# Two attention layers: each block closed one turn later, and another order in the last turn

## The chip, the cores and the metric

The kernel runs on one core of a Trainium2 chip. The metric is the device time of one execution in microseconds (us); fourteen executions of the kernel before have a median of 4657.06 us (4653.63 to 4668.51). The core's engines work side by side, each through its own queue in order: TensorE (PE, matmuls; PEld its weight loads), VectorE (DVE), ScalarE (ACT), GpSimd (POOL) and SyncE (SP, which only issues transfers). They wait for one another through semaphores.

## What is computed

Eight steps act on a table of 3125 nodes with 256 features: four graph layers and four mixtures of experts in turn. The change touches the third step alone, two graph attention layers over 50000 edges plus one loop for each node. Each layer is

```python
h = (x @ W).reshape(n_nodes, Hh, Cc)          # 4 heads of 64
a_src = (h * att_src).sum(-1)
a_dst = (h * att_dst).sum(-1)
alpha = leaky_relu(a_src[src] + a_dst[dst])
m = jax.ops.segment_max(alpha, dst, num_segments=n_nodes)
e = jnp.exp(alpha - m[dst])
denom = jax.ops.segment_sum(e, dst, num_segments=n_nodes)
w = e / jnp.clip(denom, 1e-16)[dst]
out = jax.ops.segment_sum(w[:, :, None] * h[src], dst, num_segments=n_nodes)
return out.reshape(n_nodes, Hh * Cc) + bias
```

The first layer's result goes through relu into the second; the second's is added to the table. A mixture of eight experts (two for each node) follows.

## The kernel before

Nodes are padded to 25 blocks of 128 (T = 25), and the edges are sorted by receiver, so that block b has 17 chunks of 128 edges (kb = 17, KB = 17), the last block 8. `attend` runs one attention layer; its body is `attend_blocks`. The two large layers take its branch for `small = False` (64 features a head); a third, small layer later in the program takes the other branch, which is not touched.

**The parts of a block's work** (functions inside `attend_blocks`):

- `begin` issues one gather for each chunk on POOL (`self.gather`, L373): 128 rows of the table `rows`, 260 wide, into the tile `ad_rows`, which has four buffers. On SP it loads the block's own rows (`ad_hx`, pool `ad_x`, three buffers) and the receivers' numbers (`ad_rb`).
- `hot`, `hot_t`, `hot_wide` build one-hot matrices of the receivers (DVE; `hot_wide` is an ACT copy to float32, two buffers). `to_edges` brings the receivers' logits to the edges (PE), `receivers` finishes them (DVE).
- `highest` scans the gathered logits along the chunks for the largest of each receiver (DVE, L2279 to L2287) and transposes the ends (PE, L2289). `across` scans over the 128 lanes (DVE, L2294) and transposes back (PE, L2297). `scores` makes the exponents (DVE L2302 to L2315, then ACT's exp L2316).
- `products` multiplies the gathered rows by their weights, a range of chunks at a time (DVE, L2325, four instructions, one for each head).
- `summed(x, j)` adds the products up by receiver with matmuls against the one-hot matrices (PE, L2344), two matmul records a chunk. j counts four ranges of chunks, `x.cut = [0, 2, kb // 2, kb - kb // 4, kb]`.
- `closed` divides by the sum of the weights and adds the node's own loop (DVE, L2353 to L2366, then the first instructions of `finish`). What is left of `finish` is a generator, `x.end`.

`finish` is `to_second` in layer 1: after bias and relu (L2494, L2495), `x.end` runs `heads`: two transposes on PE (L2176), a copy on ACT (L2178), four matmuls (L2182), a copy on ACT (L2184), the store of the block's new row into layer 2's table on SP (L2185), and a copy of eight columns on DVE (L2186). In layer 2 it is `to_rows`: bias and sum into the table X (L2500, L2501), and `x.end` then sends up to two routed rows on POOL (`mix_send`, L891) and advances the router of the next mixture by one `mix_step` (two in the last blocks). A router group of five blocks takes six steps: mean, variance and normalisation (the first, with L204, which writes one of two row buffers), transposes and logits (L822, L812, read on DVE by L816), the two best experts, counts (L856, L857, read by L872) and positions.

**The order.** `in_order` chains the instructions of PE, of DVE and of ACT in the order in which the program makes them, and the middle of the program is chained on POOL too; SP is not. The loop runs 26 turns. In turn b the block b is `mid` (its logits are scanned), b - 1 is `low` (its products are summed) and b + 1 is `new` (its gathers are issued, its one-hot matrices built). At the end of the turn `low` is closed, the first half of `mid`'s products is made, and `low.end` is run to its end. Between the layers POOL sends 30 records of another graph's sort (`own_send(30)`, L1968), issued behind the last block's gathers of layer 1.

Of the kernel before, what the change touches and what calls it, by code (L numbers as in the profile page):

```python
# [36 lines left out]
T = 25  # L37
# [1236 lines left out]
class Fast(Net):  # L1274
# [920 lines left out]
    def attend_blocks(self, s, C, rows, nd, finish, hxs, spare, tail, between):  # L2195
        nc, tc = self.nc, self.tc
# [3 lines left out]
        small = C < 64  # L2200
        with ExitStack() as ctx:
# [10 lines left out]
            hp = ctx.enter_context(tc.tile_pool(name="ad_h", bufs=4 if small else 2))  # L2212
            fp = None if small else ctx.enter_context(tc.tile_pool(name="ad_f", bufs=2))
            tp = ctx.enter_context(tc.tile_pool(name="ad_t", bufs=2))
            xp = None if small else ctx.enter_context(tc.tile_pool(name="ad_x", bufs=3))
            op = ctx.enter_context(tc.tile_pool(name="ad_o", bufs=2)) if small else None
            psc = ctx.enter_context(tc.tile_pool(name="ad_pc", bufs=1, space=PSUM))
            psx = ctx.enter_context(tc.tile_pool(name="ad_px", bufs=1, space=PSUM))
# [26 lines left out]
            def hot(x, j):  # L2245
                k0 = s.k0[x.b]
                for k in range(j * x.kb // 2, (j + 1) * x.kb // 2):
                    nc.vector.tensor_scalar(x.hb[:, k, :], self.iotab, s.rel[:, k0 + k:k0 + k + 1], None,  # L2248
                                            op0=OP.is_equal)

            def hot_t(x):
                nc.vector.tensor_scalar(x.hT[:, :x.kb * P], x.rb[:, :x.kb * P], self.pcol, None, op0=OP.is_equal)
# [5 lines left out]
            def to_edges(x):  # L2258

                x.px = psx.tile([P, KB, 24], F32, name="ad_px")  # L2260
                for k in range(x.kb):
                    nc.tensor.matmul(x.px[:, k, :], x.hT[:, k * P:(k + 1) * P],
                                     nb[:, x.b].rearrange("p j f -> p (j f)"), start=True, stop=True)
# [11 lines left out]
            def highest(x):  # L2275

                kb = x.kb
                v = sp.tile([P, 4, KB], F32, name="ad_v")[:, :, :kb]
                nc.vector.tensor_copy(v, x.es.rearrange("p k h -> p h k"))  # L2279
                x.F = sp.tile([P, 2, 4, KB], F32, name="ad_F")[:, :, :, :kb]  # L2280
                for h in range(4):
                    nc.vector.tensor_tensor_scan(x.F[:, 0, h, :], s.drop[:, x.ks], v[:, h, :], -BIG, OP.add, OP.max)
                for h in range(4):
                    nc.vector.tensor_tensor_scan(x.F[:, 1, h, ::-1], s.end[:, x.ks][:, ::-1], v[:, h, ::-1], -BIG,
                                                 OP.add, OP.max)
                nc.vector.tensor_copy(e[:, 0:4], x.F[:, 0, :, kb - 1])
                nc.vector.tensor_copy(e[:, 32:36], x.F[:, 1, :, 0])  # L2287
                x.two = psc.tile([P, P + 36], F32, name="ad_pt")
                nc.tensor.transpose(x.two[0:36, 0:P], e, self.ident)  # L2289

            def across(x):

                for q, out, way in ((0, slice(2, P + 2), slice(0, P)), (32, slice(P - 1, None, -1), slice(P - 1, None, -1))):
                    nc.vector.tensor_tensor_scan(c[q:q + 4, out], s.dropT[q:q + 4, x.b, way], x.two[q:q + 4, way], -BIG,  # L2294
                                                 OP.add, OP.max)
                x.pb = x.two[:, P:]
                nc.tensor.transpose(x.pb, c[:, 1:P + 1], self.ident[0:36, 0:36])  # L2297

            def scores(x):
                kb = x.kb  # L2300
                z = x.z[:, :, 0, :]
                nc.vector.tensor_tensor(z, x.es, x.ex[:, :, 4:8], OP.add)  # L2302
                nc.vector.scalar_tensor_tensor(z, z, 0.2, z, op0=OP.mult, op1=OP.max)
                q = sp.tile([P, 4, KB], F32, name="ad_q")[:, :, :kb]
                for i, far in enumerate((s.cum, s.back)):
                    nc.vector.tensor_tensor(q, x.pb[:, 32 * i:32 * i + 4, None].to_broadcast([P, 4, kb]),
                                            far[:, None, x.ks].to_broadcast([P, 4, kb]), OP.add)
                    nc.vector.tensor_max(x.F[:, i], x.F[:, i], q)
                nc.vector.tensor_max(q, x.F[:, 0], x.F[:, 1])
                top = sp.tile([P, KB, 4], F32, name="ad_top")[:, :kb, :]  # L2310
                nc.vector.tensor_max(top, q.rearrange("p h k -> p k h"), x.ex[:, :, 0:4])
                nc.vector.tensor_add(top, top, x.ex[:, :, 4:8])
                nc.vector.scalar_tensor_tensor(top, top, 0.2, top, op0=OP.mult, op1=OP.max)
                nc.vector.tensor_tensor(x.z, x.z, top[:, :, None, :].to_broadcast([P, kb, 2, 4]), OP.subtract)
                nc.vector.tensor_tensor(x.z, x.z, s.mask[:, x.ks, :, None].to_broadcast([P, kb, 2, 4]), OP.add)  # L2315
                nc.scalar.activation(x.rt[:, :kb, W4:HY], x.z.rearrange("p k i h -> p k (i h)"), AF.Exp)  # L2316
# [22 lines left out]
            def summed(x, j):  # L2339
                if j == 0:  # L2340
                    x.acc = psa.tile([P, 3 * HY if small else HY], F32, name="ad_acc")
                for k in range(x.cut[j], x.cut[j + 1]):
                    lhs, rhs = (x.hb, x.rp.rearrange("p k i f -> p k (i f)")) if small else (x.hd, x.rt)
                    nc.tensor.matmul(x.acc, lhs[:, k, :], rhs[:, k, :], start=k == 0, stop=k == x.kb - 1)  # L2344

            def closed(x):
                den = sp.tile([P, 4], F32, name="ad_den")
                o4 = sp.tile([P, 4], F32, name="ad_o4")
                tot = x.acc
                if small:  # L2350
                    tot = sp.tile([P, HY], F32, name="ad_tot")
                    nc.vector.tensor_reduce(tot, x.acc.rearrange("p (i f) -> p f i", i=3), AX.X, OP.add)
                nc.vector.tensor_reduce(den, tot[:, W4:HY].rearrange("p (i h) -> p h i", i=2), AX.X, OP.add)  # L2353
                nc.vector.scalar_tensor_tensor(o4, den, 0.5, tot[:, HX:HY], op0=OP.is_lt, op1=OP.add)
                nc.vector.scalar_tensor_tensor(den, den, 0.5, den, op0=OP.is_lt, op1=OP.add)
                if small:
                    nc.vector.tensor_scalar_add(den, den, 1e-16)
                else:
                    nc.vector.tensor_scalar_max(den, den, 1e-16)
                nc.vector.reciprocal(den, den)  # L2360
                o = op.tile([P, W4], F32, name="ad_out") if small else x.hx[:, 0:W4]
                ov = o.rearrange("p (h c) -> p h c", h=4)
                nc.vector.tensor_tensor(ov, x.hx[:, 0:W4].rearrange("p (h c) -> p h c", h=4),
                                        o4[:, :, None].to_broadcast([P, 4, C]), OP.mult)
                nc.vector.tensor_tensor(o, o, tot[:, 0:W4], OP.add)
                nc.vector.tensor_tensor(ov, ov, den[:, :, None].to_broadcast([P, 4, C]), OP.mult)  # L2366
                x.end = finish(x.b, o)
                next(x.end)
# [8 lines left out]
            if small:  # L2377
# [6 lines left out]
                for b in range(T + 3):  # L2384
                    low, second, first, new = second, first, new, None
# [37 lines left out]
                        pass  # L2423
                return
            mid = low = None
            for b in range(T + 1):
                low, mid, new = mid, new, None
                if b + 1 < T:
                    new = begin(b + 1)
                if mid:  # L2430
                    highest(mid)
                if low:
                    summed(low, 0)
                if new:
                    hot_t(new)
                    to_edges(new)
                if mid:
                    across(mid)
                if low:
                    products(low, low.cut[2], low.kb)  # L2440
                    summed(low, 1)
                if new:
                    hot(new, 0)
                if mid:
                    scores(mid)
                if new:
                    hot(new, 1)
                    hot_wide(new)
                if low:
                    summed(low, 2)  # L2450
                    summed(low, 3)
                if new:
                    receivers(new)
                if low:
                    closed(low)
                if mid:
                    products(mid, 0, mid.cut[2])
                if low:
                    for _ in low.end:
                        pass  # L2460

    def r1_gnn(self):
        nc, tc, a = self.nc, self.tc, self.a
# [487 lines left out]
```

## Time and profile before

| what | value |
|---|---|
| median of 14 executions | 4657.06 us |
| the profiled execution | 4667.21 us, its span 4665.4 us |
| busy over the span | PE 72%, DVE 66%, POOL 47%, ACT 37% |
| mean granted TensorE clock | 0.84 of full |
| layer 1: first to last gather | 1079.6 to 1624.4 us |
| layer 2: first to last gather | 1667.7 to 2249.7 us |
| one turn of layer 1, blocks 3 to 23 | 22.3 us |
| last closing (L2353), layer 1 and layer 2 | 1658.1 and 2296.2 us |

How to read the views: the page's groups give line, engine, operation, output and inputs, count, then busy us and the mean ns of one, then the engine's idle time just ahead of them and what ended it. The timeline gives start, duration, engine, line, operation and, in brackets, the idle time ahead of it and its releaser. The view by windows gives start and end of each, then for PE, PEld, DVE, ACT and POOL the busy us and instruction count, then the granted TensorE clock (1.00 is full), the DMA share and GB/s. The waits give who waited for whom: total us, times, longest.

### The profile page before, as it was taken

The numbers are of one execution on the slowest core, as the hardware profiler recorded it, in microseconds if no ns is written. First come the engines' busy times: TensorE is split into PE (matmuls) and PEld (weight loads), VectorE is DVE, ScalarE is ACT, GpSimd is POOL, SyncE is SP. The second block draws the span as 40 slices with busy tenths as digits, with TensorE's granted clock in tenths as the row PEclk, the third lists the DMA queues.
The fourth block names the chain that finished last, engine by engine and source line by source line (L and its number), as shares of the span: only waits on it lengthen the run. The fifth ranks groups of instructions, "written<-read, shape, count | busy, mean of one in ns | idle before, by whom it ended". The sixth has DMA issues, their size and how long they took to land.

```text
span 4665.4 us, 58758 instructions
## 1 busy us (share of the span) xinstructions
PE 3352.0 (72%) x17877; PEld 2696.3 (58%) x17877; DVE 3081.3 (66%) x10158; ACT 1735.4 (37%) x3743; POOL 2183.7 (47%) x2117
## 2 busy tenths in 40 slices
PE   5689977854566534444475897757688699997998
PEld 2479965743444423433354676644455489876887
DVE  8768874355777758887745787756877789643221
ACT  5736451221111101111111698733233368762221
POOL 2665545566777777777455000027777100022222
PEclk9689987976777767767687998879789799998999
DMA  2942224654554434444355222221111012355665
GB/s 58 213 131 100 100 95 152 188 161 125 139 141 138 123 103 132 131 129 126 98 174 160 71 103 86 72 55 33 38 33 35 8 60 84 119 162 169 190 190 164
DMA packets 345476, 535.49 MB, mean 115 GB/s; under 512 B 78177, under 2 KB 246881, under 8 KB 341878
## 3 DMA queue, kind: packets, MB, share of 16 engines
q1 hardware_dynamic: 249218, 372.22, 25.2%
q0 software_dynamic: 90272, 155.06, 13.7%
q10 hardware_dynamic: 5652, 4.27, 0.3%
q8 instruction: 148, 2.42, 0.2%
q14 instruction: 186, 1.52, 0.1%
HBM read 390.08 MB, written 146.81 MB: 115 GB/s over the span
## 4 chain that ended last, share of the span: by engine, by line
PE 28%; DVE 20%; POOL 14%; issue 10%; DMA 7%; ACT 6%; DVEq 0%; SPq 0%; POOLq 0%; ACTq 0%
POOL ad_rows L373 12%; PE gx_pa L1063 5%; PE gx_po L1003 4%; ACT oo_y L2043 3%; PE ad_acc L2344 3%; PE r_pa L1778 3%; DVE ad_hb L2248 2%; DVE ad_rows L2325 2%; DMA ys<-gx_ys,gx_to 2%; PE r_o L1740 2%; PE ss_sum L2716 2%; DMA ad_rows<-r_rows,fa_gi 2%; PE r_pa L1780 2%; PE r_pa L1781 1%; DMA ad_rows<-q_rows,own_gi 1%
## 5 line engine op out<-in xcount | busy, mean ns | idle before, releaser
L373 POOL DMA_INDIRECT ad_rows<-r_rows,fa_gi x832 | 842.5, 1013 | 280.1 <-issue 240.1
L1968 POOL DMA_INDIRECT os_table<-os_rec,os_at x512 | 564.1, 1102 | 483.3 <-ACT r_wt L1669 135.6
L373 POOL DMA_INDIRECT ad_rows<-q_rows,own_gi x416 | 401.4, 965 | 636.8 <-DMA q_w<-in_L_ffn_W 510.3
L2344 PE MATMUL ad_acc<-ad_rows,ad_hd 128*128 128x264 f32 x1664 | 498.2, 463 | 9.2 <-DVE ad_rows L2325 9.2
L891 POOL DMA_INDIRECT regions<-gh_xn,gd_at x150 | 152.2, 1015 | 629.6 <-PE r_pa L1778 462.7
L2289 PE MATMUL ad_pt<-ident,ad_e 128*36 128x128 f32 x75 | 26.1, 348 | 577.6 <-DVE ad_e L2287 577.6
L1064 ACT ACTIVATE gx_h<-gx_pa,gx_bias 128x256 f32<-128x256 f32 x392 | 185.5, 473 | 673.0 <-PE gx_pa L1063 672.9
L2344 PEld LDWEIGHTS ad_acc<-ad_rows,ad_hd 128*128 128x128 f32 x1664 | 374.4, 232 | 86.2 <-DVE ad_rows L2325 9.9
L1063 PE MATMUL gx_pa<-gx_xt,gx_w 128*128 128x256 f32 x1568 | 388.2, 406 | 42.9 <-DVE gx_xt L1044 40.2
L1003 PE MATMUL gx_po<-gx_w,gx_h 128*128 128x256 f32 x1568 | 371.3, 383 | 27.6 <-DVE gx_ys L1005 27.6
L1063 PEld LDWEIGHTS gx_pa<-gx_xt,gx_w 128*128 128x128 f32 x1568 | 309.9, 202 | 115.8 <-DVE gx_xt L1044 60.8
L2289 PEld LDWEIGHTS ad_pt<-ident,ad_e 128*36 128x36 f32 x75 | 7.8, 104 | 607.8 <-issue 582.1
L1003 PEld LDWEIGHTS gx_po<-gx_w,gx_h 128*128 128x128 f32 x1568 | 294.0, 192 | 70.7 <-DVE gx_ys L1005 31.4
L2316 ACT ACTIVATE ad_rows<-ad_z 128x136 f32<-128x136 f32 (+1 forms) x75 | 23.5, 314 | 805.4 <-DVE ad_z L2315 779.1
L1631 PE MATMUL r_pa<-r_xn,r_wt 128*128 128x257 f32 x1250 | 299.0, 384 | 24.4 <-ACT r_wt L1669 24.4
L2716 PE MATMUL ss_sum<-r_xw,ss_wt 128*128 128x256 f32 x1250 | 288.6, 393 | 0.6 <-DVE r_xw L2609 0.6
L1053 DVE TENSOR_TENSOR gx_to<-gx_tf,gd_other 128x2 int32<-128x2 f32 x84 | 13.5, 161 | 415.3 <-DMA ys<-gx_ys,gx_to 209.6
L2716 PEld LDWEIGHTS ss_sum<-r_xw,ss_wt 128*128 128x128 f32 x1250 | 244.8, 198 | 35.5 <-DVE r_xw L2609 1.0
L1631 PEld LDWEIGHTS r_pa<-r_xn,r_wt 128*128 128x128 f32 x1250 | 229.5, 193 | 53.0 <-ACT r_wt L1669 25.1
L2325 DVE SCALAR_TENSOR_TENSOR ad_rows<-ad_rows 128x512 f32<-128x512 f32 (+2 forms) x400 | 258.8, 709 | 1.5
L1011 POOL DMA_INDIRECT xd<-gx_ys,gx_to x56 | 86.3, 1541 | 333.3 <-DVE gx_ys L1006 267.1
L2856 PE MATMUL q_o<-q_w,q_h 128*128 128x256 f32 x800 | 203.9, 400 | 6.7 <-ACT q_ct L2824 3.4
(615 smaller groups left out, 7913.7 us busy)
## 6 DMA issues: line engine op xcount, KB each, us to landing
gx_w<-in_L_ffn_W SPq DMA_DIRECT2D x56, 1024.0 KB
mats<-r_wt SPq DMA_DIRECT2D x25, 1600.0 KB
ss_wt<-mats SPq DMA_DIRECT2D x25, 1600.0 KB
gx_w<-in_L_ffn_W SPq DMA_DIRECT2D x56, 512.0 KB
regions<-zero SPq DMA_DIRECT2D x26, 1040.0 KB
ad_rb<-fa_relT SPq DMA_DIRECT2D x48, 544.0 KB
gx_xs<-regions SPq DMA_DIRECT2D x84, 260.0 KB
cnts<-r_cb SPq DMA_DIRECT2D x75, 256.0 KB
```

The source lines that it names most:

```text
L373: return self.nc.gpsimd.indirect_dma_start(out=out, out_offset=None, in_=table[:, :], in_offset=bass.IndirectOffsetOnAxis(ap=idx, axis=0))
L891: ins = nc.gpsimd.indirect_dma_start(out=self.regions[:, :], out_offset=bass.IndirectOffsetOnAxis(ap=m.at[i][:, t:t + 1], axis=0), in_=x, ...
L1003: nc.tensor.matmul(po, h[:, f, j * P:(j + 1) * P], w2s[:, f, :], start=f == 0, stop=f == FC - 1)
L1063: nc.tensor.matmul(ps, w1s[:, c, f * P:(f + 1) * P], xt[:, c, :], start=c == 0, stop=c == DC - 1)
L1064: done = nc.scalar.activation(h[:, f, :], ps, act, bias=bias1[:, f, k:k + 1])
L1631: nc.tensor.matmul(pa, wt[:, i, :], xn[:, g * G + i, :], start=i == 0, stop=i == G - 1)
L1778: nc.tensor.matmul(pa, c[:, u - u0, :], xs[:, u, 0:2 * D], start=u == 0, stop=u == T - 1)
L1968: i = nc.gpsimd.indirect_dma_start(out=s.table[:, :], out_offset=bass.IndirectOffsetOnAxis(ap=s.at[:, c:c + 1], axis=0), in_=s.rec[:, c, : ...
L2325: i = nc.vector.scalar_tensor_tensor(rv[:, :, h, :], rv[:, :, h, :], 1.0, x.rt[:, u:v, W4 + h:W4 + h + 1].to_broadcast([P, v - u, C]), op0 ...
L2344: nc.tensor.matmul(x.acc, lhs[:, k, :], rhs[:, k, :], start=k == 0, stop=k == x.kb - 1)
L2716: nc.tensor.matmul(sums[t], wt[:, d, :], xw[:, d, :], start=d == 0, stop=d == T - 1)
L2856: nc.tensor.matmul(po, last[:, c, f * P:(f + 1) * P], w2[:, e - 1, c, :], start=c == 0, stop=c == FC - 1)
```

## The change

A block is closed one turn later: `done` is the block that was `low` in the turn before. Its closing stands behind `highest(mid)`, and its `end` behind `summed(low, 1)`. The pool `ad_x` gets a fourth buffer, since a block's own rows are held longer. In turn T - 1 (24) the two older blocks, 22 and 23, are closed and ended ahead of the scans of block 24. Of block 24 only the first two chunks' products are made in that turn, and they are summed at once; in turn T the other three ranges of chunks are multiplied and summed by turns, and the block is closed.

```diff
-            xp = None if small else ctx.enter_context(tc.tile_pool(name="ad_x", bufs=3))
+            xp = None if small else ctx.enter_context(tc.tile_pool(name="ad_x", bufs=4))
...
             mid = low = None
+            done = None
+
+            def ended(x):
+                closed(x)
+                for _ in x.end:
+                    pass
+
             for b in range(T + 1):
                 low, mid, new = mid, new, None
+                if b == T - 1:
+                    ended(done)
+                    products(low, low.cut[2], low.kb)
+                    for j in range(4):
+                        summed(low, j)
+                    ended(low)
+                    low = done = None
+                if b == T:
+                    for j in range(1, 4):
+                        products(low, low.cut[j], low.cut[j + 1])
+                        summed(low, j)
+                    ended(low)
+                    break
                 if b + 1 < T:
                     new = begin(b + 1)
-                if mid:
-                    highest(mid)
+                highest(mid)
+                if done:
+                    closed(done)
                 if low:
                     summed(low, 0)
                 if new:
                     hot_t(new)
                     to_edges(new)
-                if mid:
-                    across(mid)
+                across(mid)
                 if low:
                     products(low, low.cut[2], low.kb)
                     summed(low, 1)
+                if done:
+                    for _ in done.end:
+                        pass
                 if new:
                     hot(new, 0)
-                if mid:
-                    scores(mid)
+                scores(mid)
                 if new:
                     hot(new, 1)
                     hot_wide(new)
...
                 if new:
                     receivers(new)
-                if low:
-                    closed(low)
-                if mid:
+                if b == T - 1:
+                    products(mid, 0, mid.cut[1])
+                    summed(mid, 0)
+                else:
                     products(mid, 0, mid.cut[2])
-                if low:
-                    for _ in low.end:
-                        pass
+                done = low
```

## Prediction, on record before the result was known

> **What bounds the kernel now.** I read the page first (engines, groups), then the waits inside layer 1, then the timeline of one turn and of the last turns, then the clock by windows. The span is 4665.4 us; its execution took 4667.2 us, 10 us above the median of 4657.1, so the sum is made as a difference and added to either.
>
> The page's group of gathers of the two large layers:
>
> ```profile
> L373 POOL DMA_INDIRECT ad_rows<-r_rows,fa_gi x832 | 842.5, 1013 | 280.1 <-issue 240.1
> ```
>
> Waits of 1166 to 1612 us, twenty turns of layer 1 (total us, times, longest):
>
> ```profile
> POOL ad_rows L373 <- issue: 96.9, 318, 0.3
> DVE ad_v L2279 <- DMA ad_rows<-r_rows,fa_gi: 61.4, 20, 3.7
> DVE r_nd L2186 <- ACT hd_hx L2184: 18.8, 20, 1.5
> ```
>
> POOL never waits for anything but its own 0.3 us between two gathers. A turn lasts 22.3 us (scans of block 3 at 1170.3, of block 23 at 1616.1: 445.8 / 20) because 17 gathers take it. DVE has 3.1 us to spare a turn, idle at L2279 until the rows land, and 0.9 us at L2186. One turn:
>
> ```profile
> 1170.32 0.25 DVE L2279 COPY ad_v<-ad_rows 128x68 f32<-128x68 f32 x1 [2.97 <-DMA ad_rows<-r_rows,fa_gi]
> 1171.92 1.97 PE L2344 MATMUL ad_acc<-ad_rows,ad_hd 128*128 128x264 f32 x4
> 1172.25 0.84 DVE L2294 TENSOR_TENSOR_SCAN ad_c<-fa_dropT,ad_pt 4x128 f32<-4x128 bf16 x2
> 1173.12 2.77 DVE L2325 SCALAR_TENSOR_TENSOR ad_rows<-ad_rows 128x576 f32<-128x576 f32 x4
> 1174.51 8.69 PE L2344 MATMUL ad_acc<-ad_rows,ad_hd 128*128 128x264 f32 x30
> 1183.24 0.17 DVE L2353 TENSOR_REDUCE ad_den<-ad_acc 128x4 f32<-128x8 f32 x1 [0.30 <-PE ad_acc L2344]
> 1188.94 0.17 DVE L2186 COPY r_nd<-hd_ps 128x8 f32<-128x8 f32 x1 [0.31 <-ACT hd_hx L2184]
> ```
>
> PE fills 1171.9 to 1183 without a hole. Its clock, around the scans of block 8 (1281.3), is half and then full:
>
> ```profile
> 1281.30:1287.30 6.00, 4.58 (x27) 3.60 (x28) 5.89 (x22) 0.00 (x0) 4.78 (x5) 0.50 0.63 191
> 1287.30:1297.50 10.20, 6.42 (x29) 4.95 (x28) 9.48 (x42) 2.32 (x2) 7.76 (x9) 1.00 0.39 106
> ```
>
> The end of layer 1, where DVE, not POOL, sets the pace:
>
> ```profile
> 1635.18 0.19 DVE L2279 COPY ad_v<-ad_rows 128x32 f32<-128x32 f32 x1 [0.20 <-issue]
> 1647.48 0.17 DVE L2353 TENSOR_REDUCE ad_den<-ad_acc 128x4 f32<-128x8 f32 x1 [4.29 <-PE ad_acc L2344]
> 1658.11 0.17 DVE L2353 TENSOR_REDUCE ad_den<-ad_acc 128x4 f32<-128x8 f32 x1 [3.13 <-PE ad_acc L2344]
> 1664.51 0.32 SPq L2185 DMA_DIRECT2D r_rows<-hd_hx  x1
> 1667.68 0.99 POOL L373 DMA_INDIRECT ad_rows<-r_rows,fa_gi  x1 [2.68 <-PE ad_px L2262]
> ```
>
> Layer 2 cannot gather until the last block's rows are stored (L2185).
>
> **Part 1, the interior of layer 1.** What goes: DVE's wait at L2353 for the last sums, 2.1 us over twenty turns. It stands beside POOL's gathers, so it buys nothing. What moves: the closing (L2353 to L2495, 1183.24 to 1186.14 = 2.9 us) goes in between the scans and hot_t; its end (two transposes, copy, four matmuls, copy, store on SP, L2186) goes in behind summed(low, 1) on PE, and L2186 in front of hot(new, 0) on DVE. DVE, ACT and PE run in program order, so every product, score and scan queues behind L2186.
>
> DVE from the scans' start: scans 1.2, closing to 4.1, hot_t to 4.9 (0.81), across to 5.8 (0.84), second products to 8.5 (2.77). Then it waits for L2186. PE meanwhile: the first four matmuls end at 3.6 (1171.92 + 1.97), then nothing to do until hot_t at 4.9; to_edges to 5.7, and the transpose behind across to 6.2. Only then the twelve matmuls of summed(low, 1). The trace has them starting 0.44 us apart at half clock and 0.22 at full. In the twenty turns the clock rose 4.8 to 8.1 us after the scans' start, that is 3.2 to 6.5 us after PE was filled (1.6). Filled without a hole only from 5.0 or 5.9, it should rise between 8.2 and 12.4; I take 10.5. By then ten of the twelve are out; the sums end at 11.2 (bounds: all full 8.9, all half 11.6). The end's chain takes 2.6 (1186.37 to 1188.94) at full clock, 3.5 (1631.27 to 1634.81) at half. So L2186 starts at 13.8 (11.5 to 15.1) and DVE waits 5.3 us (3.0 to 6.6) where it waited 0.9.
>
> Turn: 22.3 - 3.1 - 0.9 - 0.1 (L2353) + 0.2 (least idle at L2279, 1635.18) + 5.3 = 23.7, against POOL's 22.3. DVE becomes the bound by 1.4 us; with the bounds, from -0.9 (hidden) to +2.7. Turns 2 to 22 have an older block to end: 21 x 1.4 = **29 us** (0 to 57). The four row buffers let POOL run ahead: block b+1 needs the sums of b-3, which end a turn and more earlier even then.
>
> [...]
>
> **Part 2, the end of layer 1.** Now: scans of 23 at 1616.1, L2185 at 1664.5, 48.4 us. Then, from the scans of 23 (kb of 24 is 8): L2186 at 13.7, hot 0.7, scores 3.3, hot 0.7, receivers 0.8, products 2.5: 21.7. Turn 24 closes 22 (2.9) and waits out its end chain (3.5): 28.1; second products of 23 (2.8) stand beside the 34 matmuls of 23, which start at 27.5 behind the chain and take 9.5 (30 took 8.66 at 1638.8): 37. Closing and end of 23: 43.1. Only now the scans of 24, alone: 1.2, transpose 0.7, across 0.8, transpose 0.5, scores 2.8, exp 0.3: 49.4 (today they run while PE sums 23). First products 0.9, sixteen matmuls 5.3 to 6 (5.29 at 1652.8; the parts hide the rest of the products): 56. From L2353 to the store 6.4 (1658.11 to 1664.51): 62.4. **+14 us** (11 to 17). The cover is gone on POOL too: its 30 own_sends ended at 1665.0, so each later us of L2185 is idle POOL; in the other direction they cap a gain at 2.4 us.
>
> **Part 3, layer 2.** No L2186, but one mix_step stands where the end is. Idle-free turns, by the step that they hold (scan starts 1831.0, 1849.0, then less idle): 18.0, 18.2, 18.7, 22.6, 31.9. Three of five have L816, which now never waits (11 times, idle 0); behind summed(low, 1) and eight matmuls (0.95) it would start at 12.2, after 8.5: +3.7. The fifth waits for the counts' matmuls: +2.5. POOL's turn is 22.3, then 25.1 once two sends of routed rows go in (2.6 + 0.3); a step later means one pair fewer before the last gathers, -2.9. A wait that exists stays: L204 reuses a row buffer whose sends stand behind the next block's gathers:
>
> ```profile
> 2062.78 1.49 DVE L204 TENSOR_TENSOR gh_xn<-X,ln_m 128x1280 f32<-128x1280 f32 x1 [4.16 <-DMA regions<-gh_xn,gd_at]
> ```
>
> Walk on layer 2's own times: turn 6 starts at 1824.7 (block 6's last gather ends at 1822.7, its scans follow such an end by 2.0); with the first step 28.6, then 18.0, 21.9, 22.4, 26.3, 34.4 and 18.0, 21.9, 22.4, 26.3: turn 16 at 2064.9. L204 is reached 16.2 later, and waits until 2085.6 (block 17's gathers 2084.2 - 2.9, sends 2.6, landing 1.7): 34.4 + 4.5. Then 88.6, and 34.4 + 3.4, and 18.0: block 23 scans at 2248.2, not 2238.4. **+10 us** (2 to 18). Its tail, from those scans: turn 24 starts at 19.3, closing of 22 to 22.3, second products to 25.1, nine chunks of sums to 30, closing of 23 to 33, mix steps 17.3 (2273.5 to 2290.8 now) to 50.3, scans to exp 6.3, first products 0.9, sixteen matmuls 5.3 to 6.5: last closing at 64 after those scans, not 57.75 (2238.40 to 2296.15): **+6** (3 to 10).
>
> **Edits at nothing.** The fourth ad_x buffer: its load on SP waits for the end of b-3 in turn b-1, as now for b-2; a whole turn covers it, and without cover 2 us once. The store L2185 leaves SP mid-turn; no later SP transfer of the turn waits for it. Sixteen small products instead of eight: 3.5 against 2.8 us, beside the sums.
>
> **Sum.** 29 + 14 + 10 + 6 = 59: 4726 on the profiled execution's scale, **4716** on the median's.
>
> **Rivals.** A, the interior stays under POOL: if the hole costs PE no clock, L2186 starts at 11.5 to 12.3, the turn is 21.4 to 22.2, and parts 2 and 3 remain: 14 + 16 = 4687. For it: DVE's 3.1 us spare; against: the clock rose late after every pause. B, not slower: the last turn with the older blocks first costs nothing. That decides if block 24's rows land after block 23 has closed; by the trace their last gather ends at 1624.4, and block 23 closes at 1647.5. If it were so, layer 1 gains 2.4 (POOL's cap), layer 2 2.9 for the send pair and 1 to 2 for the parts: 4651. C, PE stays at half clock through the interior: wait 6.6, 57 + 14 + 26 (layer 2 near its upper bounds) = 97: 4754. D, that the change removes no wait, is half true and in the sum: the waits at L2353 are off the path.
>
> **Chances.** Main 0.62 (its own range 4697 to 4745), A 0.20, C 0.10, B 0.08. From A's lower bounds to C: 4680 to 4756. 0.2% is 9.3 us, about what a measurement tells from no change; B alone lies within or below: faster 0.03, same 0.05, slower 0.92.
>
> **What would show it.** After: L2186's idle 5 us, with L2279's near 0 in layer 1; clock rise 8 to 12 us after the scans; layer 1's turns 23.7; POOL idle some 40 us before layer 2; L816 waiting 3 to 4 us; scans of 24 behind L2186 of 23. Wrong if L2279 keeps waiting for rows in layer 1 (A), or if the scans of 24 wait for rows (B).

## The result, and the profile after

The changed kernel takes 4699.83 us (median of 6 executions, 4697.47 to 4706.68); the kernel before, on the same chip, 4656.27 (28 executions). The ratio is 1.0095, its 95% interval 1.0085 to 1.0105: slower by 44 us. The profiled execution of after took 4701.7 us, its span is 4699.8.

The two layers, cut at the same events in both profiles (us):

| from ... to | before | after | difference | predicted |
|---|---|---|---|---|
| layer 1's first gather, scans of block 23 | 536.5 | 561.7 | +25.2 | +29 |
| ... layer 2's first gather | 51.6 | 64.8 | +13.2 | +14 |
| ... scans of block 23 in layer 2 | 570.7 | 579.3 | +8.6 | +10 |
| ... last closing of layer 2 | 57.8 | 62.4 | +4.6 | +6 |

Layer 1 first. In the groups and in the waits of twenty of its turns (1169.5 to 1640; total us, times, longest), POOL goes on as it did, with 0.3 us between gathers, and DVE's wait has moved from L2279, which is no longer in the list, to L2186:

```profile
L373 POOL DMA_INDIRECT ad_rows<-r_rows,fa_gi x832 | 839.0, 1008 | 317.2 <-issue 237.4
```

```profile
DVE r_nd L2186 <- ACT hd_hx L2184: 107.0, 20, 5.7
POOL ad_rows L373 <- issue: 98.4, 323, 0.3
...
PE ad_px L2262 <- DVE ad_hT L2252: 28.5, 20, 1.5
```

One of these turns in the timeline (start, duration, engine, line, and in brackets the idle time ahead):

```profile
1404.09 0.25 DVE L2279 COPY ad_v<-ad_rows 128x68 f32<-128x68 f32 x1
...
1405.29 0.16 DVE L2353 TENSOR_REDUCE ad_den<-ad_acc 128x4 f32<-128x8 f32 x1
...
1405.69 2.06 PE L2344 MATMUL ad_acc<-ad_rows,ad_hd 128*128 128x264 f32 x4
...
1408.41 0.78 DVE L2252 TENSOR_SCALAR ad_hT<-ad_rb,pcol 128x2176 bf16<-128x2176 bf16 x1
...
1409.25 0.63 PE L2262 MATMUL ad_px<-ad_nb,ad_hT 128*128 128x24 bf16 x17 [1.50 <-DVE ad_hT L2252]
...
1410.26 5.65 PE L2344 MATMUL ad_acc<-ad_rows,ad_hd 128*128 128x264 f32 x12
...
1418.39 0.17 DVE L2186 COPY r_nd<-hd_ps 128x8 f32<-128x8 f32 x1 [5.65 <-ACT hd_hx L2184]
```

The closing (L2353 on) stands ahead of hot_t, PE pauses 1.50 us, the twelve matmuls take 5.65 us, and L2186 starts 14.3 us after the scans. The same turn by windows of the clock's own grid (start and end; PE's busy us are the first figure behind the length, the granted clock the 1.00 or 0.50):

```profile
1405.75:1409.17 3.42, 2.00 (x5) 1.05 (x4) 3.21 (x10) 0.00 (x0) 2.81 (x3) 0.50 0.42 116
1409.17:1412.58 3.41, 3.20 (x23) 2.56 (x24) 3.35 (x7) 0.00 (x0) 2.49 (x4) 0.50 0.73 223
1412.58:1416.00 3.42, 3.42 (x10) 2.48 (x8) 0.17 (x1) 0.00 (x0) 2.81 (x3) 0.50 0.44 127
1416.00:1419.40 3.40, 2.88 (x14) 2.30 (x13) 1.00 (x7) 0.75 (x2) 2.49 (x4) 1.00 0.52 136
```

The clock rises behind the first window that PE filled whole, 11.9 us after the scans, when all twelve matmuls have gone at half clock: behind 3.20 busy us of 3.41 it was still at half, behind 3.42 of 3.42 it was full. In layer 1 of this profile (1150 to 1650 us) all 22 rises stand behind a half-clock window that PE filled to 96% or more, and none of the 62 half-clock windows without a rise behind them was filled over 97%. The grid is read from the traces: in the profiles of before and after, all changes of the granted clock stand whole multiples of 3.41 us apart.

How far DVE falls back is seen best by setting each block's scans against the end of its last gather: in layer 1 of before the scans come 2.1 to 3.1 us behind it up to block 23; after, 3.9 us at block 3, 11.7 at block 10, 17.7 at 16, 28.2 at 23. POOL's own pace is unchanged (block 23's last gather ends 534.2 and 533.5 us behind the first one), so what DVE loses comes due at the end of the layer:

```profile
1661.20 0.16 DVE L2353 TENSOR_REDUCE ad_den<-ad_acc 128x4 f32<-128x8 f32 x1
...
1675.84 0.17 DVE L2353 TENSOR_REDUCE ad_den<-ad_acc 128x4 f32<-128x8 f32 x1 [4.75 <-PE ad_acc L2344]
...
1683.08 0.19 DVE L2279 COPY ad_v<-ad_rows 128x32 f32<-128x32 f32 x1 [0.21 <-issue]
...
1694.90 0.17 DVE L2353 TENSOR_REDUCE ad_den<-ad_acc 128x4 f32<-128x8 f32 x1 [2.89 <-PE ad_acc L2344]
1701.19 0.32 SPq L2185 DMA_DIRECT2D r_rows<-hd_hx  x1
...
1704.31 0.99 POOL L373 DMA_INDIRECT ad_rows<-r_rows,fa_gi  x1 [40.82 <-PE ad_px L2262]
```

Closings of 22 and 23, scans and closing of 24, its store, and layer 2's first gather behind 40.82 us of idle POOL (2.68 before). In layer 2, L816 now waits (its line's answer: us, times), and L204, which waited 4.16 us at the same step before:

```profile
L816 DVE COPY gh_lg<-hd_ps x12: 158/174/176, 1919.0 to 2315.9; 128x16 f32<-128x16 f32 x8, 128x8 f32<-128x8 f32 x4
...
  PE hd_ps L812: 31.2, 10
```

```profile
2120.49 1.49 DVE L204 TENSOR_TENSOR gh_xn<-X,ln_m 128x1280 f32<-128x1280 f32 x1 [8.97 <-DMA regions<-gh_xn,gd_at]
```

The four differences make 51.6 us, 8 more than the medians do, and 17.2 more than the two spans differ (34.4). These 17.2 us lie outside the two layers: 1.8 ahead of layer 1; 1.7 from the last closing of layer 2 to the next mixture's first product (36.7 us before, 35.0 to 35.1 in the four profiles with the new last turn); 8.2 in that mixture's products (182.6 us in the profile of before, 174.4 after, and 170.1 to 175.9 in three kernels below that leave them alone); 5.5 behind them. There is one profile of each kernel, so the four rows below are good to some us only; why those products differ between profiles is not known.

### The profile page after: what moved, and what is told of

The parts are those of the page before. It is cut to its first block, busy times and chain, and to the rows that moved or that the text cites. A ratio compares the mean times of both kernels' runs of the same rounds, so it can differ in the third digit from the quotient of the medians.

```text
span 4699.8 us, 58786 instructions
## 1 busy us (share of the span) xinstructions
PE 3382.8 (72%) x17877; PEld 2705.6 (58%) x17877; DVE 3086.2 (66%) x10174; ACT 1737.5 (37%) x3743; POOL 2180.0 (46%) x2117
## 4 chain that ended last, share of the span: by engine, by line
PE 31%; DVE 22%; POOL 11%; issue 8%; DMA 6%; ACT 6%; DVEq 0%; SPq 0%; POOLq 0%; ACTq 0%
POOL ad_rows L373 9%; PE ad_acc L2344 5%; PE gx_pa L1063 5%; PE gx_po L1003 4%; ACT oo_y L2043 3%; PE r_pa L1778 3%; DMA ys<-gx_ys,gx_to 2%; DVE ad_hb L2248 2%; PE r_o L1740 2%; DVE ad_rows L2325 2%; PE ss_sum L2737 2%; PE r_pa L1780 2%; PE r_pa L1781 1%; DMA ad_rows<-r_rows,fa_gi 1%; DMA ad_rows<-q_rows,own_gi 1%
## 5 line engine op out<-in xcount | busy, mean ns | idle before, releaser
L2344 PE MATMUL ad_acc<-ad_rows,ad_hd 128*128 128x264 f32 x1664 | 547.3, 494 | 10.1 <-issue 9.8
L2344 PEld LDWEIGHTS ad_acc<-ad_rows,ad_hd 128*128 128x128 f32 x1664 | 397.8, 247 | 98.3 <-ACT ad_rows L2316 7.7
L2867 PE MATMUL q_a<-q_xT,q_w 128*128 128x512 f32 (+1 forms) x448 | 195.9, 568 | 4.4 <-ACT q_h L2870 4.4
```

Of the source, the lines that this page charges most:

```text
L2867: nc.tensor.matmul(ps[:, :n * P], w1[:, e, c, f * P:(f + 1) * P], xT[:, c, t0 * P:(t0 + n) * P], start=c == 0, stop=c == DC - 1)
```

## The experiments

Times are set against runs of the kernel before on the same chip. The second group of four ran where the kernel before takes 4641.13 us (21 runs). The first and third groups came to chips where it takes 5315.83 (16 runs) and 5259.95 (18): engines stand still there for microseconds within a turn (last section), so these eight runs answer their questions only in part. The four rows of the table, for the kernels of the second group (no profile of before was taken with that group, so the column is the one above):

| us | before | after | act_copy_2 | no_hole_2 | tail_only_2 | best24 |
|---|---|---|---|---|---|---|
| layer 1 to scans of 23 | 536.5 | 561.7 | 535.3 | 533.3 | 538.6 | 539.2 |
| to layer 2's first gather | 51.6 | 64.8 | 59.7 | 61.0 | 56.1 | 46.3 |
| layer 2 to scans of 23 | 570.7 | 579.3 | 578.5 | 583.7 | 568.4 | 568.4 |
| to the last closing | 57.8 | 62.4 | 63.5 | 59.3 | 60.6 | 50.9 |
| sum against before | | +51.6 | +20.4 | +20.7 | +7.1 | -11.8 |
| measured, ratio to before | | 1.0095 | 1.0043 | 1.0045 | 1.0017 | 0.9986 |

**The wait itself: L2186 on ACT.** The changed kernel, with the copy that DVE stood at made elsewhere, in layer 1's heads:

```diff
-        nc.vector.tensor_copy(nd[:, t, :], ps[:, D:D + 8])
+        (nc.scalar.copy if on_act else nc.vector.tensor_copy)(nd[:, t, :], ps[:, D:D + 8])
...
-                yield from self.heads(psp, tp, we2, o, rows[1], nd[1], b)
+                yield from self.heads(psp, tp, we2, o, rows[1], nd[1], b, True)
```

> The changed kernel with L2186, the copy of the eight columns at the end of layer 1's chain, made on ACT instead of DVE; the pause on PE stays, layer 2 stays as changed. Theory (what lengthens layer 1's turns is that DVE stands behind L2186, all else has time): DVE reaches hot(new, 0) at 8.6 us after the scans instead of 14.4, waits for rows again (3 us or more at L2279), turns of 22.3 us: 25 us come back, and up to 5 in turn 24, where the same wait stood: 4673 (4666 to 4680). Rival, the wait was only where the lateness showed, and the next step stands just as late behind PE or ACT (the exponents on ACT, the second sums on PE): 4690 or more, with the wait at L2325 or L2353 instead.

> The kernel with L2186 on ACT once more, for a chip on which the kernel before takes its usual 4650 to 4670 us (the first time it came to one that takes 5316, where engines stand still for microseconds in the middle of a turn). There layer 1 went from 686 us (blocks closed in their own turn) to 627, so DVE's wait was the path. Theory: on the usual chip POOL's 22.3 us are the floor of a turn, so layer 1 only comes back to it: L2279 waits for rows again, 3 us or more, and the time is 25 us, at most 30, under that of the changed kernel: before + 14 to + 20, 4670 to 4676. Rival, DVE without both waits lets the turn fall under 22.3 us as it did on the other chip: at or below the time of before.

On the usual chip 4662.67 us against 4641.13, ratio 1.0043 (1.0026 to 1.0059), +20 us: half the loss is gone. In the profiles 26.4 us of it come back in layer 1's interior and 5.1 at its end; layer 2 stays as changed. DVE's wait list in some twenty turns has the rows again and no L2186, and a turn takes 22.3 us, POOL's pace:

```profile
DVE ad_v L2279 <- DMA ad_rows<-r_rows,fa_gi: 80.7, 19, 4.7
DVE ad_v L2279 <- issue: 9.7, 2, 4.9
```

The pause on PE is still there (1.26 us) and the clock still rises late (8.8 to 12.0 us after the scans), but nothing on DVE stands behind it. The floor also holds from below: DVE is idle 4.3 us a turn at L2279 and layer 1 takes 535.3 us, as before (536.5). On the other chip (first run) layer 1's turns take 25.0 us and DVE does not wait for rows in them; the ratio was 0.9958 (0.9945 to 0.9971), so there the late closing, without the wait, gains.

**The pause on PE: the closing behind across.** DVE has the same work ahead of L2186 in another order:

```diff
                 highest(mid)
-                if done:
-                    closed(done)
...
                 across(mid)
+                if done:
+                    closed(done)
```

> The changed kernel with one step moved: the late closing stands behind across instead of ahead of hot_t, so DVE does the same work in the same time up to L2186, but hot_t and across come early enough that PE goes from the first sums to to_edges, the second transpose and the next sums without a pause. Theory (the pause of 1.5 us on PE delays the rise of its clock, the sums, the heads and L2186): the clock rises 4.8 to 8.1 us after the scans as before, L2186 starts near 11.5 instead of 14.2, DVE waits 3.0 us instead of 5.6, its turn is 21.4 us and layer 1 goes back to POOL's 22.3: 25 us of layer 1 come back, 4675 (4668 to 4682). Rival, the clock does not matter and it is the 2.9 us of closing and the chain behind the sums alone: L2186 still starts at 13.5 or later, 4692 or more.

> The kernel with the late closing behind across once more, for the usual chip. On the other chip layer 1 took 748 us with it and 756 without, so the pause on PE was worth 8 us of 70 there. Theory: on the usual chip PE has no pause, its clock rises 4.8 to 8.1 us after the scans, L2186 starts near 11.5, DVE waits 3 us there and again at L2279: layer 1's turns are 22.3 us and 25 us come back: before + 15 to + 22. Rival (the chain behind the sums makes the wait, the clock little of it): L2186 starts at 13.5 or later, turns of 23 us or more, before + 35 or more.

4660.41 us, ratio 1.0045 (1.0029 to 1.0060), +21 us. One turn, and two windows of it:

```profile
1356.06 0.22 DVE L2279 COPY ad_v<-ad_rows 128x68 f32<-128x68 f32 x1 [2.14 <-DMA ad_rows<-r_rows,fa_gi]
...
1357.63 2.06 PE L2344 MATMUL ad_acc<-ad_rows,ad_hd 128*128 128x264 f32 x4
1358.80 0.17 DVE L2353 TENSOR_REDUCE ad_den<-ad_acc 128x4 f32<-128x8 f32 x1
...
1359.48 0.66 PE L2262 MATMUL ad_px<-ad_nb,ad_hT 128*128 128x24 bf16 x17
...
1360.32 4.61 PE L2344 MATMUL ad_acc<-ad_rows,ad_hd 128*128 128x264 f32 x12
...
1367.31 0.17 DVE L2186 COPY r_nd<-hd_ps 128x8 f32<-128x8 f32 x1 [2.65 <-ACT hd_hx L2184]
```

```profile
1360.30:1363.70 3.40, 3.40 (x9) 2.66 (x9) 3.30 (x7) 0.00 (x0) 2.57 (x3) 0.50 0.61 203
1363.70:1367.10 3.40, 2.88 (x14) 2.25 (x13) 0.96 (x2) 0.57 (x2) 2.71 (x3) 0.99 0.54 143
```

PE runs through, the clock rises 5.6 to 8.2 us after the scans (4.8 to 8.1 before, 8.7 to 12.0 after), L2186 starts at 11.05 in the median of turns 2 to 22 (14.2 with the change; near 11.5 was expected), DVE waits there 2.4 us instead of 5.6, and rows are waited for again. The twelve matmuls start 4.3 us after the scans instead of 6.2 and take 4.3 us instead of 5.6 (medians of twenty turns): the pause on PE was worth 1.9 us by itself and 1.3 by the clock, 3.2 on DVE, and that decided whether DVE stayed under POOL's turn. In layer 2, of which the expectation says nothing, none of the 8.6 us came back: 583.7 us. DVE's waits from layer 2's first gather to the scans of block 23, first with the change, then here:

```profile
DVE ad_v L2279 <- DMA ad_rows<-r_rows,fa_gi: 51.1, 7, 19.7
DVE gh_lg L816 <- PE hd_ps L812: 28.5, 9, 4.0
DVE gh_xn L204 <- DMA regions<-gh_xn,gd_at: 15.2, 2, 9.0
```

```profile
DVE ad_v L2279 <- DMA ad_rows<-r_rows,fa_gi: 67.3, 11, 19.6
DVE gh_xn L204 <- DMA regions<-gh_xn,gd_at: 28.0, 2, 14.1
DVE ad_v L2279 <- issue: 8.1, 3, 3.5
...
DVE gh_lg L816 <- PE hd_ps L812: 4.6, 6, 1.3
```

L816's waits went from 28.5 us to 4.6; at L204 12.8 us came back, and at L2279 23.9 (0.4 <- issue with the change). One of the two waits at L204:

```profile
2076.70 1.01 POOL L891 DMA_INDIRECT regions<-gh_xn,gd_at  x1 [0.30 <-issue]
2078.02 0.99 POOL L891 DMA_INDIRECT regions<-gh_xn,gd_at  x1 [0.30 <-issue]
2080.66 1.49 DVE L204 TENSOR_TENSOR gh_xn<-X,ln_m 128x1280 f32<-128x1280 f32 x1 [14.12 <-DMA regions<-gh_xn,gd_at]
```

L204 waits for sends that POOL issues between gathers, in POOL's time. It starts 2.6 us behind the start of the second send here, and 2.6 to 2.7 in the profiles of before and after. What DVE saves ahead of it, it waits at it, or for rows. On the other chip this kernel stayed at 1.0117 (1.0099 to 1.0136): the waits at L2186 last 10 us there in the median of twenty turns.

**The last turns alone, the interior alone.** For the first, blocks are closed in their own turn, and only from turn 24 on the order is the new one; for the second, the late closing runs through turn 24 and the end is the old one:

```diff
                 if b == T - 1:
-                    ended(done)
                     products(low, low.cut[2], low.kb)
...
+                if low:
+                    closed(low)
                 if b == T - 1:
                     products(mid, 0, mid.cut[1])
                     summed(mid, 0)
                 else:
                     products(mid, 0, mid.cut[2])
-                done = low
+                if low:
+                    for _ in low.end:
+                        pass
```

```diff
-                if b == T - 1:
-                    ended(done)
+                if b == T:
+                    summed(low, 0)
                     products(low, low.cut[2], low.kb)
-                    for j in range(4):
-                        summed(low, j)
-                    ended(low)
-                    low = done = None
-                if b == T:
                     for j in range(1, 4):
-                        products(low, low.cut[j], low.cut[j + 1])
                         summed(low, j)
                     ended(low)
...
                 if b == T - 1:
-                    products(mid, 0, mid.cut[1])
-                    summed(mid, 0)
-                else:
-                    products(mid, 0, mid.cut[2])
+                    closed(low)
+                products(mid, 0, mid.cut[2])
+                if b == T - 1:
+                    for _ in low.end:
+                        pass
```

> Only the last turns of the change: each block is closed in its own turn as before, and from turn 24 on block 23 is multiplied, summed, closed and ended ahead of the scans of block 24, whose products come in parts. Theory: +13 at the end of layer 1 (POOL idle some 40 us ahead of layer 2's first gather, 2.7 before) and +5 at the end of layer 2, together +18: 4674 (4668 to 4680). Rival, the order of the last turn costs nothing by itself, and the 13 us come from the late closing of block 22 in it: +5 or less, below 4662.

> The kernel with the last turns of the change alone, once more for the usual chip (on the other it took 0.3% more than before, 16 us). Theory: +13 at the end of layer 1 with POOL idle some 40 us ahead of layer 2's first gather, +5 at the end of layer 2: before + 14 to + 20, layer 1's turns 22.3 us. Rival, the late closing of block 22 is what costs there: before + 5 or less.

> Only the interior of the change: blocks are closed a turn later through turn 24, and the last turn has the order of before (block 23 is closed at the end of turn 24, block 24 in turn 25). Theory: the two parts add up, and the interior carries most. Layer 1's interior measured +25 us and layer 2's +9 in the profile of the changed kernel, so 34 in all; in turn 24 one closing more (2.9 us) and L2186 of block 22 stand ahead of the scores of block 24, +2 to +5 in each layer: 4690 to 4700, with layer 1's turns at 23.5 us. Rival, the last turn is what costs and the interior is hidden under POOL: +5 to +10, 4661 to 4666, with turns of 22.3 us.

The last turns alone: 4646.94 us against 4641.13, ratio 1.0017 (1.0007 to 1.0027), +6 us by the medians and +8 by the ratio, where 14 to 20 were expected. Layer 1's end takes 56.1 us, so 4.5 of the 13.2 come from the new order itself:

```profile
1623.74 0.17 DVE L2353 TENSOR_REDUCE ad_den<-ad_acc 128x4 f32<-128x8 f32 x1 [6.11 <-PE ad_acc L2344]
...
1630.79 0.47 DVE L2279 COPY ad_v<-ad_rows 128x32 f32<-128x32 f32 x1 [0.21 <-issue]
...
1652.32 1.00 POOL L373 DMA_INDIRECT ad_rows<-r_rows,fa_gi  x1 [7.62 <-DVE ad_hb L2248]
```

POOL idles 7.6 us, not 40: most of the 40 with the change is DVE's lag out of the interior, 28.2 us behind the rows of block 23 there and 2.2 here. The other 8.7 us are the late closing's share in these turns: L2186's wait in turn 23, and block 22's closing and chain in turn 24 (act_copy_2 and no_hole_2, which shorten or lose the wait, stand between with 59.7 and 61.0). So the expectation's split of the end into "last turns" and "interior" was wrong, and its rival half right. In layer 2 the scans of 23 stand 2.1 us behind their rows here as in before, 15.3 in after. The interior alone ran on the other chip only: ratio 1.0130 (1.0099 to 1.0162), with the last turns alone 1.0030 (1.0012 to 1.0049) there. On the usual chip what the last turns alone leave of the whole loss, 44 - 8 = 36 us, says the same if the two parts add up: the interior carries most.

**Three runs that met the slower chip.** The late block's end at the end of the turn; late closing only up to block 18; and the kernel before with 4.8 us more DVE work a turn:

```diff
-                if done:
-                    for _ in done.end:
-                        pass
                 if new:
                     hot(new, 0)
...
                     products(mid, 0, mid.cut[2])
+                if done:
+                    for _ in done.end:
+                        pass
```

> The changed kernel with the late block's end (layer 1: heads, store, L2186; layer 2: sends and mix_step) at the end of the turn instead of behind summed(low, 1); the closing stays ahead of hot_t, with the pause on PE. Layer 1, my theory: nothing stands behind L2186 any more, turns of 22.3 us, 25 us come back. Layer 2: the prediction's terms were DVE's waits at L816 and L872 (+3.7 and +2.5 a group of five blocks); they go with this edit. By them layer 2's first gather to the scans of block 23 falls back to 571 to 573 us and the kernel is at before + 14 to + 17. Rival for layer 2, seen when the scans of each block are set against the landing of its last gather: the group's heavy first step (L204) simply runs one turn later, in turn 21 instead of 20, and DVE has one turn fewer to catch up with POOL before the last blocks; then L816 no longer waits, yet scans of 23 still stand 10 us or more behind their rows (2 before, 15 with the change), layer 2 stays at 578 to 584: before + 20 to + 25.

```diff
                 if b == T - 1:
-                    ended(done)
...
+                if T - 5 <= b < T - 1:
+                    closed(low)
...
+                if T - 5 <= b < T - 1:
+                    for _ in low.end:
+                        pass
+                    low = None
                 done = low
```

> The changed kernel, where the late closing ends with block 18: in turn 20 block 18 is closed late and block 19 at the end of the same turn, and from there each block is closed in its own turn; the last two turns are the changed ones without block 22's closing. If layer 2's loss is the heavy step of the group 15 to 19 coming one turn late (turn 21), this undoes it and keeps all other late steps with their waits at L816: scans of 23 stand 2 to 5 us behind their rows, layer 2 to the scans of 23 at 569 to 573 us. If the waits at L816 in the fifteen turns before are what costs, it stays at 576 or more. Layer 1: 16 late turns instead of 21 at 1.2 us more each, +19, caught up by nothing since DVE has no idle time to give back but 3 us a turn: +8 to +15 at the scans of 23; last turns +7 as with the last turns alone. Total: before + 15 to + 24 by the first, + 22 to + 30 by the second.

```diff
+                if between and 2 < b < T - 2:
+                    for _ in range(6):
+                        hot_t(new)
```

> The kernel before with six more instructions of hot_t's kind (L2252, 0.79 us each by the trace, writing the same values once more) at the end of each of layer 1's turns 3 to 22: 4.8 us more DVE work. Theory: DVE has 2.9 us a turn to give (idle 3.1 at L2279, 0.2 remains), POOL's 22.3 hide that; the rest, 1.9 us, lengthens each turn to 24.2: 20 turns, before + 36 to + 40. Rival, DVE's work is on the path in full: + 96; or POOL's row buffers hide more of it: + 20 or less. What lies behind layer 2 is unchanged here and should take what it takes in the profile of before (182.6 us from the first to the last product of the next mixture's experts) if that is its time, or 174 to 178 as in the other profiles if the profile of before was a slow one there.

Ratios 1.0073 (1.0052 to 1.0093), 1.0105 (1.0083 to 1.0128) and 1.0028 (1.0011 to 1.0045). The expectations were sums over POOL's 22.3 us; layer 1's turns are 27.0, 30.3 and 28.1 us here, so none of the three sizes is tested, and DVE's slack under POOL was not measured by itself. Layer 2 says a little: with on_time the scans of block 23 stand 31.2 us behind their rows, as with the last turns alone on such a chip (31.5); with end_late 52.8, with the interior alone 42.4. So on this chip the lag at the end is larger where block 19's heavy step runs in turn 21. But layer 2's times do not follow it (707.3, 704.7, 722.2 and 697.5 us in this order). What the usual chip shows of that step stands under part 3 below.

**A kernel under before.** The blocks are closed in their own turn; in turn 24 the last block's products and sums go ahead of the closing of 23, and 24 of the 30 records are sent between the layers:

```diff
-            for b in range(T + 1):
+            for b in range(T):
...
+                if b == T - 1:
+                    products(mid, 0, mid.cut[2])
+                    summed(mid, 0)
+                    summed(mid, 1)
+                    products(mid, mid.cut[2], mid.kb)
+                    summed(mid, 2)
+                    summed(mid, 3)
+                    ended(low)
+                    ended(mid)
+                    break
...
-between=lambda: self.own_send(30))
+between=lambda: self.own_send(24))
```

> A kernel of my own, from the kernel before: blocks closed in their own turn; only in turn 24 block 24's products are all made, and its sums follow block 23's on PE, ahead of the closing of block 23, so that DVE does not wait 4.3 and 3.1 us at L2353; and of the 30 records that POOL sends between the layers 24 are sent there and 6 later. Theory: the last store of layer 1 comes 5 us sooner and POOL is not in the way, layer 2's end is 6 us shorter: before - 7 to - 12. Rival, the six records cost as much where they now stand, or the ends of the blocks are not on the path: within 3 us of before.

> The kernel with block 24's products and sums ahead of block 23's closing (0.14% under before), with two edits more: L2186 on ACT in layer 1, since DVE still waited 2.1 us at it before it could close block 24, and 26 of the 30 records between the layers instead of 24 (POOL stood idle for 6.0 us there, a record takes 1.27). Theory: the scans of 23 to layer 2's first gather take 44 us instead of 46.3, and two records fewer stand in the mixture: before - 8 to - 12. Rival, no more than measured: before - 4 to - 7.

best24 takes 4634.36 us against 4641.13, ratio 0.9986 (0.9977 to 0.9995): faster, by 6.5 us where 7 to 12 were expected. The layers give 11.8 in the profiles; what of the rest the six later records cost is not settled. DVE no longer waits for sums at either closing:

```profile
1634.05 0.17 DVE L2353 TENSOR_REDUCE ad_den<-ad_acc 128x4 f32<-128x8 f32 x1
...
1640.04 0.15 DVE L2353 TENSOR_REDUCE ad_den<-ad_acc 128x4 f32<-128x8 f32 x1
...
1649.94 0.99 POOL L373 DMA_INDIRECT ad_rows<-r_rows,fa_gi  x1 [6.01 <-PE ad_px L2262]
```

best26 (L2186 on ACT as well, 26 records) ran on the slower chip: 5239.87 us against 5259.95, ratio 0.9959 (0.9943 to 0.9975). Its gain on the usual chip was not measured.

## Why the prediction was right

**The total.** 4716 was forecast, 4680 to 4756; 4699.8 came. The likeliest case is the one that happened. The sum was 59 us; the four profiled rows make 51.6, each term having been 0.8 to 3.8 too large, and the medians 44. The 8 us between the last two belong to stretches outside the two layers, as said above, and are not explained.

**Part 1, layer 1's interior: mechanism right, and shown.** L2186's start 14.2 us after the scans in the median (13.8 said), wait 5.6 (5.3), clock rise 11.8 in the median (10.5, bounds 8.2 to 12.4), turn 23.5 (23.7), L2279's wait gone; 25.2 us for 29. Taking away the wait alone, or the pause alone, brings the whole of it back. PE is refilled 5.2 us after the scans, and a window of the grid of 3.41 us that lies wholly behind that ends 8.6 to 12.0 us after the scans; the twenty rises came at 8.7 to 12.0.

**Part 2, the end of layer 1: right step by step.** From the scans of 23, said and measured: L2186 13.7 and 14.1; closing of 22 21.7 and 21.7; its chain done 28.1 and 28.8; closing of 23 37 and 36.4; block 24's exponents done 49.4 and 49.2; last closing 56 and 55.4; store 62.4 and 61.7.

**Part 3, layer 2: right by L204, not by L816.** Said: L816 +3.7 in three of five turns, L872 +2.5, L204's wait 4.5 and 3.4. Measured: L816 2.5 to 4.0, L872 1.3 to 1.6, L204 9.0 and 6.3. The terms for L816 and L872 are not what makes the 10: the walk itself runs into L204, whose start POOL sets, and there they come off the wait again. In turn 21 the walk has L204 at 2212.0, which is 544.3 us behind the layer's first gather, and the scans of block 23 36.2 us later; measured are 542.9 and 36.3. no_hole_2 shows it: without most of the waits at L816 the scans of block 23 stand as far behind their rows, 15.1 us against 15.3.

What the prediction left unsaid is why that costs. L204's start lies 4.3 us behind the last gather of the next block in all five profiles here (before, after, act_copy_2, no_hole_2, tail_only_2): block 21's in turn 20 before and with the last turns alone, block 22's in turn 21 in the other three. From there to the next scans it is 8.8 us before, where the step stands at the end of a turn, and 18.2 with the change, where it stands in the middle. So the scans of blocks 20 to 23 stand 2.1, 13.1, 5.7 and 2.1 us behind their rows before, 6.6, 7.4, 22.5 and 15.3 with the change, and 2.1, 2.0, 22.5 and 15.1 in no_hole_2: more lag, one turn later, and one turn fewer to catch up. So the scans of block 23 stand 13.2 us further behind; less 4.7 by which its last gather ends sooner (564.0 us behind the first, 568.7 before; 20 sends go ahead of it instead of 22, and the gathers themselves take 413.0 us instead of 415.8), that makes the 8.6 to a tenth. The tail's +6 was +4.6.

**Rivals.** A (hidden under POOL) did not occur, but its condition was the right one: no_hole_2, where the pause itself is gone, comes near it with L2186 at 11.05 and turns of 22.2 us, and lies at +21 where A had +30. B and C did not occur; the scans of 24 wait for DVE's order, not for rows. D holds as said: the waits at L2353 were off the path but for the last two, which best24 removes.

## What to carry to other kernels

In an engine's fixed order, moving work later moves whatever waits for its result into the middle of other work: look for the instruction at the end of the moved chain, and ask who queues behind it. Here a pause on PE cost its length and then the clock: 1.5 us of pause became 3.2 us for the engine that waited. Before counting a wait that comes or goes, find the next wait on that engine that another engine paces; up to there, time saved is only waited elsewhere, and what counts is how much work stands behind that wait in its turn.

## What the runs showed of the hardware that was not expected

The same kernels take 13 to 15% longer on the slower chips, and most of it lies where rows are gathered. With the last turns alone, layer 1 to the scans of 23 takes 538.6 us on one chip and 685.8 on another, layer 2 to its scans of 23 568.4 and 704.7, and a later stretch that holds the small layer's gathers 556.4 and 858.5: 586 of the 688 us by which the two spans differ. A stretch of matrix products without these gathers takes 440.3 and 440.2 (440.3 in the profile of before too, L2716). On the slower chip engines stop within a turn though their inputs are there:

```profile
1507.06 0.32 PE L2297 MATMUL ad_pt<-ident,ad_c 36*128 36x36 f32 x1
...
1516.92 0.23 DVE L2306 TENSOR_TENSOR ad_q<-ad_pt,fa_cum 128x68 f32<-128x68 f32 x1 [6.26 <-PE ad_acc L2344]
...
1518.60 0.98 POOL L373 DMA_INDIRECT ad_rows<-r_rows,fa_gi  x1 [4.13 <-issue]
```

DVE stands 6.26 us ahead of L2306, whose input came 9.5 us earlier, and POOL 4.13 us between two gathers; for 2.4 us both stand, while PE works through most of DVE's stop (4.30 of the 6.00 us from 1510.9 on). The packets of the gathers themselves are as long as on the usual chip (170 ns in the mean on the slower one with the last turns alone, 6265 packets in 33.2% of the 16 DMA engines' time over 200 us of layer 1; 171 ns in the profile of before, 7341 in 39.2%). What stops the engines was not found. So a ratio does not carry from one chip to another: the change with L2186 on ACT is 0.4% faster than before there, and 0.4% slower on the usual one.
